# Four graph layers on one core: per-edge numbers summed with a stored 0/1 matrix in place of vector reductions and dots

## The chip, the core and the metric

The kernel runs on one core of a Trainium2 chip. The metric is the device time of one execution in microseconds (us), as the median of several runs; the profile is of one more execution. The engines are PE (matmul, with PEld for the weight loads), DVE (vector), ACT (scalar, activation functions), POOL (general purpose; it also issues the indirect DMAs) and SP (here it issues plain DMAs).

## What is computed

`x` has N = 2708 rows (nodes) of 512 features, `adj` is 2708 × 2708 with about five non-zero weights in a row (diagonal included). Four layers follow each other, each closed by a residual sum and a layernorm:

```python
# layer 0
x = layernorm(x + (x - (adj @ x) * (diag_1 + 1)) @ W + bias)
# layer 1: two gates, an attention over the edges
gate_a = sigmoid(concat([adj @ x, x]) @ Wa.T + ba)       # one number per row
gate_b = sigmoid(concat([adj @ x, x]) @ Wb.T + bb)
h = x @ W_sa
s = (h @ a_left)[:, None] + (h @ a_right)[None, :]       # one number per edge
e = where(adj != 0, exp(-leaky_relu(s, 0.01)), 0)
x_a = (e / (e.sum(1, keepdims=True) + 1e-5)) @ h
x_b = adj @ (x @ W_gcnb) + b_gcnb
x = layernorm(x + sigmoid(gate_a * x_a + gate_b * x_b))
# layer 2
head = (adj > 0) / max(norm of its row, 1e-12);  inc = adj + head
x = layernorm(x + (inc @ x) / inc.sum(1, keepdims=True))
# layer 3
A = adj + I;  d = A.sum(0) ** -0.5
x = layernorm(x + tanh((d[:, None] * A * d[None, :]) @ x @ W3.T + b3))
```

## The kernel before

The rows are worked on in 22 blocks of 128 (the last has 20); `xs` keeps all of x in SBUF, block by block. Everything takes place in `sparse_path` (a dense version runs only if the adjacency doesn't fit the sparse one). The edges of a block, up to 640, are put into five tiles of 128 edges. An edge has its value `ev`, its column `ej` (the row of x to fetch) and its row within the block `ec`; a sixth "tile" is the block's own rows, with the diagonal values.

`gather` (L606) fetches the 128 x-rows of each tile by one indirect DMA on POOL's queue: five a block in every layer, into a ring of eleven buffers. `one_hot` (L624) makes of a tile's edge numbers the matrix s[edge, row] = value where the row is the edge's, by one DVE instruction a tile, six a block. `aggregate` (L635) multiplies the six matrices with the gathered rows on PE (one 128x512 matmul each), and so sums the edges by row. `dot` (L640) is a DVE product with a row sum. `transposed` (L647, L649) is four PE transposes and an ACT copy, `project` (L654) four matmuls with a 512 × 512 weight, `layernorm` is L662 to L673, and `store` issues on SP, as the adjacency load (L701) does.

**Layer 0** also finds the edges. The loop at L903 to L915 works at three blocks at once: in pass `it` it loads adjacency block it+1 (double buffered, SP's queue), finds the non-zeros of block `it` (Max8 and FindIndex8, L766 and L767, with ACT's `minus` passes at L773, which test for negative values), moves the found numbers of block it−1 to edge tiles (`spread_rows`: matmuls `got` L829, ACT copies `rowsets` L839) and reads values and columns off them (`pick_edges`: `hit` L848, `prod` L852, `e` L859, far, num, `ej` L866, `row` L870), after which it issues the gathers, and projects block it−2: `l0a` (aggregate), `l0u` (L882, L883), transposes, `l0o` (POOL's `xb` L879 by the identity at L890, then `project`), layernorm, a dot with `wr` for the attention, and the store of x1 with that number behind it (`x1d`). After the loop come a test of the adjacency and the column degrees `deg` and `d_inv` (L942 to L966), which layer 3 needs.

**Layers 1 to 3** share the loop `layer` (L1078): gather block i+1, prepare its matrices, then compute block i and finish block i−1. In layer 1 `l1_prepare` (L984 to L1045) makes three dots of the block's rows, spreads the left attention number by a PE transpose (`sp`) and an ACT copy, picks it per edge with a 128x768 product and a row reduction (`tmp` L1001, L1010), adds the gathered right numbers, max, leaky ReLU, Exp, makes the second matrix `se`, and sums the columns of three such matrices (attention, value, count) by a `part` reduction over tiles (L1026, L1029, L1033) and three fp32 matmuls with ones (`sums` L1038). `l1_gates` (L1047) makes the two gates by dots on the aggregated rows; `l1_finish` projects (`l1o`, eight matmuls) and normalises.

Each engine runs its own list of instructions in order. The order in those lists is not the program text's: a scheduler arranges the instructions ahead of time by their dependencies, and a wait stands in front of an instruction wherever a buffer or an operand comes from another engine.

Of the kernel before, what the change touches and what calls it, by code (L numbers as in the profile page):

```python
# [480 lines left out]
def sparse_path(  # L481
# [11 lines left out]
    XW = D + 2  # L493
# [19 lines left out]
    x1d = dram.tile([N, XW], FP, name="x1d")  # L513
# [6 lines left out]
    n_xg = 11  # L520
    xg_buf = [const.tile([P, XW], FP, name=f"xg{k}") for k in range(n_xg)]
    for t in xg_buf:
        nc.gpsimd.memset(t, 0.0)
# [58 lines left out]
    ej = const.tile([P, NB, TILES], U32, name="ej")  # L582
    for i in range(NB):
        nc.gpsimd.tensor_copy(ec[:, i, n_tiles(i) : n_tiles(i) + 1], iota_p)
        nc.gpsimd.tensor_copy(ev[:, i, n_tiles(i) : n_tiles(i) + 1], dval[:, i : i + 1])

    junk = const.tile([P, D], FP, name="junk")
    wl_bc = const.tile([P, D], FP, name="wl_bc")
    wr_bc = const.tile([P, D], FP, name="wr_bc")
# [8 lines left out]
    n_gathers = [0]  # L598

    def gather(i, src, width):  # L600

        tiles = []
        for t in range(n_tiles(i)):
            g = xg_buf[n_gathers[0] % n_xg]
            n_gathers[0] += 1
            nc.gpsimd.indirect_dma_start(  # L606
                out=g[:, :width],
                out_offset=None,
                in_=src[:, :],
                in_offset=bass.IndirectOffsetOnAxis(ap=ej[:, i, t : t + 1], axis=0),  # L610
                bounds_check=N - 1,
                oob_is_err=False,
            )
            tiles.append(g)
        return tiles

    def one_hot(i, vals, tag, name, diag=None):

        r = rows(i)
        nt = n_tiles(i)  # L620
        s = spool.tile([P, TILES + 1, P], FP, tag=tag, name=name)
        for t in range(nt + 1):
            v = vals[:, t : t + 1] if diag is None or t < nt else diag
            nc.vector.tensor_scalar(  # L624
                s[:, t, :r], iota_c[:, :r], ec[:, i, t : t + 1], v, op0=ALU.is_equal, op1=ALU.mult
            )
        return s

    def aggregate(pool, i, s, tiles, tag, name):
        r = rows(i)  # L630
        nt = n_tiles(i)
        agg = pool.tile([P, D], FP, tag=tag, name=name)
        for t in range(nt + 1):
            rhs = tiles[t][:, :D] if t < nt else xs[:, i, :D]
            nc.tensor.matmul(agg[:r, :], lhsT=s[:, t, :r], rhs=rhs, start=(t == 0), stop=(t == nt))  # L635
        return agg
# [107 lines left out]

    found = c0.tile([P, NB, 3, SLOTS], FP, name="found")
    index = c0.tile([P, NB, SLOTS], U32, name="index")
    count = c0.tile([P, NB, SLOTS], FP, name="count")
# [3 lines left out]
    wlr = c0.tile([P, 2, DB], FP, name="wlr")  # L751
    for s, w_bc in enumerate((wl_bc, wr_bc)):
        ps = psa.tile([P, D], FP, tag="o", name=f"wlr_ps{s}")
        for f in range(DB):
            dot(wlr[:, s, f : f + 1], w_sa_sb[:, f, :], a_bc[:, s * D : (s + 1) * D], P)
            nc.tensor.transpose(
                ps[:, f * P : (f + 1) * P], wlr[:, s, f : f + 1].to_broadcast([P, P]), ident
            )
        nc.scalar.copy(w_bc, ps)

    def find(i, a, segs):
        for s in segs:
            lo, hi = SEGS[s]
            part = a[:, lo:hi, :].rearrange("p b i -> p (b i)")
            best = found[:, i, 1, 8 * s : 8 * s + 8]
# [3 lines left out]
    def find_first(i, a):  # L769
# [11 lines left out]
        find(i, a, range(0, 3))  # L781

    def find_rest(i, a):
        find(i, a, range(3, len(SEGS)))
        f = found[:, i]
# [3 lines left out]
            count[:, i, :], ones[:, :SLOTS], valid, 0.0, op0=ALU.mult, op1=ALU.add  # L789
# [10 lines left out]
        ps = psg.tile([P, 2], FP, tag="off", name=f"off_ps{i}")  # L800
        n = count[:, i, SLOTS - 1 : SLOTS]
        nc.tensor.matmul(ps[:, 0:1], lhsT=before, rhs=n, start=True, stop=True)
        nc.tensor.matmul(ps[:, 1:2], lhsT=before2, rhs=n, start=True, stop=True)
        off = w0p.tile([P, 2], FP, tag="off", name=f"off{i}")
        nc.scalar.copy(off, ps)
        return valid, off

    def spread_rows(i, prepared):

        valid, off = prepared  # L810
        nt = n_tiles(i)
        f = found[:, i]
# [5 lines left out]
            f[:, 0, :], count[:, i, :], off[:, 0:1], valid, op0=ALU.add, op1=ALU.mult  # L818
# [4 lines left out]
            count[:, i, SLOTS - 1 : SLOTS],  # L823
# [21 lines left out]
    def pick_edges(i, rowsets):  # L845
# [25 lines left out]
        nc.vector.tensor_copy(ec[:, i, :nt], row[:, :nt])  # L871
        nc.vector.tensor_copy(ev[:, i, :nt], e2[:, :nt, 0])
        tiles = gather(i, x, D)
        return one_hot(i, ev[:, i], "s", f"s0_{i}"), tiles
# [19 lines left out]
    def l0_norm(i, o):  # L894
        r = rows(i)
        layernorm(xs[:r, i, :D], o[:r, :], r, f"l0_{i}")
        dot(xs[:r, i, D : D + 1], xs[:r, i, :D], wr_bc[:r, :], r)
        store(x1d, i, xs[:r, i, :])
# [4 lines left out]
    for it in range(NB + 2):  # L903
# [3 lines left out]
        if it < NB:  # L907
            find_first(it, adj)
# [3 lines left out]
        if it < NB:  # L912
            prepared = find_rest(it, adj)
        if o is not None:
            l0_norm(it - 2, o)  # L915


    worst = small.tile([P, 4], FP, tag="worst", name="worst")
    nc.vector.memset(worst, 0.0)
    nc.vector.tensor_reduce(  # L920
        worst[:, 0:1],
        found[:, :, 1, :].rearrange("p i (s k) -> p i s k", k=8)[:, :, :, 7],
# [4 lines left out]
    tot = psg.tile([P, NB], FP, tag="off", name="tot")  # L927
    nc.tensor.matmul(tot, lhsT=ones, rhs=count[:, :, SLOTS - 1], start=True, stop=True)
    nc.vector.tensor_reduce(worst[:, 2:3], tot[:, :NF], AX.X, ALU.max)
    nc.vector.tensor_scalar(  # L930
        worst[:, 2:3], worst[:, 2:3], float(TILES * P), None, op0=ALU.is_gt
    )
    nc.vector.tensor_scalar(worst[:, 3:4], tot[:, NF : NF + 1], float(P), None, op0=ALU.is_gt)
# [3 lines left out]
    bad_ps = psg.tile([P, NB], FP, tag="off", name="bad_ps")  # L937
    nc.tensor.matmul(bad_ps[:, 0:1], lhsT=ones, rhs=bad[:, 1:2], start=True, stop=True)
    nc.vector.tensor_scalar(flag_i, bad_ps[0:1, 0:1], 0.0, None, op0=ALU.is_gt)


    deg = c0.tile([P, NB], FP, name="deg")  # L942
    block = c0.tile([P, NB, SLOTS], U32, name="block")
    nc.vector.tensor_scalar(block, index, 7, None, op0=ALU.logical_shift_right)
    part = c0.tile([P, NB, SLOTS], FP, name="deg_part")
    dsum = c0.tile([P, len(SEGS)], FP, name="dsum")
    for m in range(4):
        nc.vector.scalar_tensor_tensor(
            part, block, float(m), found[:, :, 1, :], op0=ALU.is_equal, op1=ALU.mult
        )  # L950
        nc.vector.tensor_reduce(
            dsum, part.rearrange("p i (s k) -> p s i k", k=8), AX.XY, ALU.add
        )
        for s, (lo, hi) in enumerate(SEGS):
            if lo + m < hi:
                nc.vector.tensor_copy(deg[:, lo + m : lo + m + 1], dsum[:, s : s + 1])
    nc.vector.scalar_tensor_tensor(deg, dval, 1.0, deg, op0=ALU.add, op1=ALU.add)

    zero = c0.tile([P, NB], FP, name="zero")
    nc.vector.tensor_scalar(zero, deg, 0.0, None, op0=ALU.is_equal)  # L960
    nc.vector.tensor_add(d_inv, deg, zero)
    nc.scalar.activation(d_inv, d_inv, AF.Sqrt)
    nc.vector.reciprocal(d_inv, d_inv)
    nc.vector.tensor_scalar(zero, zero, -1.0, 1.0, op0=ALU.mult, op1=ALU.add)
    nc.vector.tensor_mul(d_inv, d_inv, zero)
    nc.vector.scalar_tensor_tensor(dd3, dval, 1.0, d_inv, op0=ALU.add, op1=ALU.mult)  # L966
# [9 lines left out]
    wa2_bc = load_row(c1, wa, "wa2_bc", off=D)  # L976
    wb2_bc = load_row(c1, wb, "wb2_bc", off=D)
    ba_bc = load_row(c1, ba, "ba_bc", n=1)
    bb_bc = load_row(c1, bb, "bb_bc", n=1)
    wa1_bc = load_row(c1, wa, "wa1_bc")  # L980
    wb1_bc = load_row(c1, wb, "wb1_bc")
    bg_bc = load_row(c1, b_gc, "bg_bc")

    def l1_prepare(i, tiles):  # L984
        r = rows(i)
        nt = n_tiles(i)
        x1 = xs[:r, i, :D]
        loc = w1p.tile([P, 4], FP, tag="loc", name=f"loc{i}", bufs=3)
        dot(loc[:r, 0:1], x1, wl_bc[:r, :], r)
        dot(loc[:r, 1:2], x1, wa2_bc[:r, :], r)  # L990
        dot(loc[:r, 2:3], x1, wb2_bc[:r, :], r)
        sp = psm.tile([P, P], FP, tag="s", name=f"sp{i}")
        nc.tensor.transpose(
            sp[:, :r], loc[:r, 0:1].to_broadcast([r, P]), ident[:r, :r]
        )
        row = w1p.tile([P, P], FP, tag="row", name=f"row_sl{i}")
        nc.scalar.copy(row[:, :r], sp[:, :r])
        sv = one_hot(i, ev[:, i], "s", f"s1v{i}")
        m = nt + 1
        tmp = w1p.tile([P, TILES + 1, P], FP, tag="tmp", name=f"tmp{i}")  # L1000
        nc.vector.scalar_tensor_tensor(  # L1001
            tmp[:, :m, :r],
            sv[:, :m, :r],
            0.0,
            row[:, None, :r].to_broadcast([P, m, r]),
            op0=ALU.not_equal,
            op1=ALU.mult,
        )
        e = w1p.tile([P, 2, TILES + 1], FP, tag="e", name=f"e{i}")
        nc.vector.tensor_reduce(e[:, 0, :m], tmp[:, :m, :r], AX.X, ALU.add)  # L1010
        for t in range(nt):
            nc.vector.tensor_add(e[:, 0, t : t + 1], e[:, 0, t : t + 1], tiles[t][:, D : D + 1])
        nc.vector.tensor_add(e[:, 0, nt:m], e[:, 0, nt:m], xs[:, i, D : D + 1])
# [216 lines left out]
```

## Time and profile before

| | |
|---|---|
| median of 3 runs | 1303.86 us (1302.4 to 1307.16) |
| the profiled execution, its own time | 1311.38 us |
| its span in the trace | 1309.7 us |
| PE, DVE, ACT, POOL busy | 82%, 70%, 37%, 39% of the span |
| the chain that ended last | PE 49%, DVE 21%, DMA 20%, issue 6%, POOL 2%, ACT 2% |
| granted PE clock, mean | 0.931 |

The span runs from the first to the last instruction of the trace. Layer 0 takes it up to about 489 us, layer 1 to 925, layer 2 from 931 to 1090, layer 3 to the end. "Busy" is a share of the whole span; since the four layers have different limits, each has to be looked at by itself. A chain of waits is read from its end backwards: each piece is what the next one waited for.

### The profile page before, as it was taken

What the parts mean: (1) busy time and instruction counts of PE and PEld (TensorE: products, weight loads), DVE (VectorE), ACT (ScalarE), POOL (GpSimd) and SP (SyncE); (2) the same over time, 40 slices, a digit from 0 to 9 for tenths busy, and PEclk for the clock granted to TensorE, in tenths of its full rate; (3) what the DMA queues carried; (4) which work ended last, traced back from release to release, by engine and by line L of the source; (5) the groups of instructions that cost most, each with busy time, mean ns of one, the idle gap of its engine ahead of it and who ended that gap; (6) DMA issues with size and microseconds to landing.
All of it is one profiled execution on the core that took longest, in us unless ns stands there. A gap on an engine that the chain in (4) does not pass through costs nothing.

```text
span 1309.7 us, 11436 instructions
## 1 busy us (share of the span) xinstructions
PE 1080.0 (82%) x2868; PEld 490.4 (37%) x2868; DVE 912.5 (70%) x2710; ACT 487.7 (37%) x820; POOL 513.2 (39%) x566
## 2 busy tenths in 40 slices
PE   0377877777778758999999999999688886999996
PEld 0233333333333314444444444444223222444442
DVE  1877786777777987988888888874477772344443
ACT  0423323233232213545445445445212111565555
POOL 5333342333424325222222222210377775755540
PEclk9989988888787977999999999999799997999999
DMA  9544544535444224222212222210366664645530
GB/s 319 132 134 129 166 131 120 157 94 168 124 125 122 78 94 112 64 65 81 67 57 83 67 57 81 66 35 16 106 196 188 184 193 125 176 146 150 147 113 36
DMA packets 111155, 154.05 MB, mean 118 GB/s; under 512 B 17214, under 2 KB 74082, under 8 KB 111082
## 3 DMA queue, kind: packets, MB, share of 16 engines
q0 software_dynamic: 35952, 96.16, 25.7%
q1 hardware_dynamic: 72364, 51.55, 12.9%
q10 hardware_dynamic: 2766, 5.55, 1.3%
q8 instruction: 25, 0.41, 0.1%
q14 instruction: 48, 0.39, 0.1%
HBM read 152.96 MB, written 22.21 MB: 134 GB/s over the span
## 4 chain that ended last, share of the span: by engine, by line
PE 49%; DVE 21%; DMA 20%; issue 6%; POOL 2%; ACT 2%; POOLq 0%; ACTq 0%; SPq 0%
PE l3a L635 9%; PE l1o L654 8%; DMA xg<-in_x_dram,ej 7%; PE l1a L635 6%; DMA xg<-x2d,ej 6%; PE l3o L654 6%; PE l0a L635 6%; DMA adj<-in_adj_dram 5%; PE l1e L635 5%; DVE junk L640 3%; PE l2a L635 3%; DVE s1e L624 2%; DVE part L1026 2%; PE l0o L654 2%; DVE index L767 2%
## 5 line engine op out<-in xcount | busy, mean ns | idle before, releaser
L606 POOL DMA_INDIRECT xg<-x1d,ej x106 | 109.6, 1034 | 271.8 <-PE l1e L635 232.9
L635 PE MATMUL l0a<-xg,s 128*128 128x512 f32 x212 | 122.2, 687 | 38.2 <-DMA xg<-in_x_dram,ej 36.4
L606 POOL DMA_INDIRECT xg<-in_x_dram,ej x106 | 107.8, 1017 | 90.1 <-DVE row L870 52.8
L606 POOL DMA_INDIRECT xg<-x3d,ej x106 | 107.5, 1014 | 78.7 <-PE l3a L635 47.0
L635 PE MATMUL l2a<-xg,s2i 128*128 128x512 f32 x212 | 110.0, 637 | 29.3 <-DMA xg<-x2d,ej 28.8
L606 POOL DMA_INDIRECT xg<-x2d,ej x106 | 115.6, 1090 | 44.6 <-issue 16.8
L654 PE MATMUL l0o<-w_sb,uT_l 128*128 128x512 f32 (+1 forms) x176 | 116.0, 821 | 13.1 <-ACT uT_l L649 12.7
L635 PE MATMUL l3a<-xg,s 128*128 128x512 f32 x212 | 100.8, 608 | 10.6 <-DMA xg<-x3d,ej 10.6
L635 PE MATMUL l1a<-xg,s1v 128*128 128x512 f32 x212 | 97.8, 608 | 8.5 <-DMA xg<-x1d,ej 8.5
L766 DVE MAX8 found<-adj 128x8 f32<-128x512 f32 (+1 forms) x132 | 82.5, 637 | 31.6 <-DMA adj<-in_adj_dram 31.3
L635 PE MATMUL l1e<-xg,s1e 128*128 128x512 f32 x212 | 99.2, 598 | 0.0
L624 DVE TENSOR_SCALAR s<-iota_c,ec,ev 128x128 f32<-128x128 f32 x234 | 69.9, 364 | 34.9 <-PE l3a L635 34.9
L654 PE MATMUL l1o<-w_gc_sb,uT_l1a 128*128 128x512 f32 (+1 forms) x176 | 85.2, 612 | 0.0
L767 DVE FIND_INDEX8 index<-found,adj 128x8 uint32<-128x512 f32 (+1 forms) x132 | 84.0, 638 | 0.0
L654 PE MATMUL l3o<-w_sb,uT_l 128*128 128x512 f32 (+1 forms) x176 | 80.3, 600 | 0.3 <-ACT uT_l L649 0.3
L879 POOL TENSOR_TENSOR xb<-xs,b_bc 128x512 f32<-128x512 f32 (+1 forms) x22 | 29.8, 1355 | 127.1 <-PE l0o L890 127.1
L654 PE MATMUL l1o<-w_sa_sb,uT_l1e 128*128 128x512 f32 (+1 forms) x176 | 79.4, 593 | 0.0
L773 ACT ACTIVATE minus<-adj 128x1408 bf16<-128x1408 f32 x44 | 60.8, 1382 | 47.5 <-DMA adj<-in_adj_dram 46.6
L635 PEld LDWEIGHTS l2a<-xg,s2i 128*128 128x128 f32 x212 | 36.3, 195 | 94.7 <-DMA xg<-x2d,ej 65.7
L654 PEld LDWEIGHTS l0o<-w_sb,uT_l 128*128 128x128 f32 (+1 forms) x176 | 44.1, 263 | 72.2 <-issue 54.1
L635 PEld LDWEIGHTS l0a<-xg,s 128*128 128x128 f32 x212 | 38.2, 208 | 86.4 <-DMA xg<-in_x_dram,ej 62.4
L635 PEld LDWEIGHTS l1a<-xg,s1v 128*128 128x128 f32 x212 | 39.3, 194 | 56.8 <-issue 44.1
(213 smaller groups left out, 1923.4 us busy)
## 6 DMA issues: line engine op xcount, KB each, us to landing
adj<-in_adj_dram SPq DMA_DIRECT2D x21, 1344.0 KB
x1d<-xs SPq DMA_DIRECT2D x21, 257.0 KB
xs<-in_x_dram ACTq DMA_DIRECT2D x3, 1792.0 KB
x2d<-xs SPq DMA_DIRECT2D x21, 256.0 KB
x3d<-l2y SPq DMA_DIRECT2D x21, 256.0 KB
out_dram<-y SPq DMA_DIRECT2D x21, 256.0 KB
xg<-in_x_dram,ej POOLq DMA_INDIRECT x106, 5.4
xg<-x1d,ej POOLq DMA_INDIRECT x106, 3.4
```

The costliest lines, as they stand in the source:

```text
L606: nc.gpsimd.indirect_dma_start(out=g[:, :width], out_offset=None, in_=src[:, :], in_offset=bass.IndirectOffsetOnAxis(ap=ej[:, i, t : t + 1 ...
L624: nc.vector.tensor_scalar(s[:, t, :r], iota_c[:, :r], ec[:, i, t : t + 1], v, op0=ALU.is_equal, op1=ALU.mult)
L635: nc.tensor.matmul(agg[:r, :], lhsT=s[:, t, :r], rhs=rhs, start=(t == 0), stop=(t == nt))
L640: nc.vector.scalar_tensor_tensor(junk[:r, :], a, 1.0, b, op0=ALU.mult, op1=ALU.mult, accum_out=acc)
L654: nc.tensor.matmul(o[:r, :], lhsT=uT[:, f, :r], rhs=w[:, f, :], start=start and f == 0, stop=stop and f == DB - 1,)
L766: nc.vector.max(out=best, in_=part)
L767: nc.vector.max_index(index[:, i, 8 * s : 8 * s + 8], best, part)
L773: nc.scalar.activation(minus, a[:, k * half : (k + 1) * half, :], AF.Relu, scale=-1.0, accum_out=neg[:, i, k : k + 1],)
L879: nc.gpsimd.tensor_tensor(xb[:r, :], xs[:r, i, :D], b0_bc[:r, :], ALU.add)
L1026: nc.vector.tensor_reduce(part[:, 0, :r], se[:, :m, :r].rearrange("p t i -> p i t"), AX.X, ALU.add)
```

## The change

1. **A stored 0/1 matrix.** In layer 0 each block's `pick[edge, row]` (bf16, 1 where the edge belongs to the row) is made once, by one DVE is_equal over 128x640, and kept for all layers. `weighted` takes the place of `one_hot`: one DVE product of `pick` with the five columns of edge values (128x640), and one ACT copy of the identity scaled by the diagonal values.
2. **Numbers per row.** After layer 0's layernorm the block is transposed and multiplied with a 512 × 6 weight: right attention number, the two gates' numbers for the aggregated side, left attention number, the two gates' numbers for the own side (`l0_columns`). `x1d` carries the first three behind the row, `sld` is a second store with the left number alone. The dot with `wr` goes.
3. **Layer 1 per edge.** Five more indirect DMAs a block fetch the left number of each edge's row (4 bytes each) by the index `er`. The attention, the value, the count and the value times each gate number are five numbers per edge; they are split into three bf16 parts and summed by row with five matmuls of `pick` (128x15). The gates, row sums and counts come out of that, before the block is aggregated.
4. The gather buffers are two of five tiles each in place of a ring of eleven; `deg` and `d_inv` are worked out at the start of layer 1; the copy of the found values goes to ACT; the total that the adjacency test needs comes from the offsets rather than from a matmul; some tags move to other pools.

```diff
-    xg_buf = [const.tile([P, XW], FP, name=f"xg{k}") for k in range(n_xg)]
+    xg_buf = [const.tile([P, TILES, XG], FP, name=f"xg{k}") for k in range(2)]
+    sl_buf = [const.tile([P, TILES], FP, name=f"sl{k}") for k in range(2)]
...
+    pick = const.tile([P, NB, TILES, P], BF, name="pick")
...
     def gather(i, src, width):
+        g = xg_buf[i % 2]
         for t in range(n_tiles(i)):
+            gather_rows(g[:, t, :width], src, ej[:, i, t : t + 1])
+        return g
...
-    def one_hot(i, vals, tag, name, diag=None):
...
-        for t in range(nt + 1):
...
-            nc.vector.tensor_scalar(
-                s[:, t, :r], iota_c[:, :r], ec[:, i, t : t + 1], v, op0=ALU.is_equal, op1=ALU.mult
-            )
+    def weighted(i, vals, pool, name, diag=None):
...
+        nc.vector.tensor_tensor(
+            s[:, :nt, :r],
+            pick[:, i, :nt, :r],
+            vals[:, :nt, None].to_broadcast([P, nt, r]),
+            ALU.mult,
+        )
+        nc.scalar.activation(
+            s[:, nt, :r],
+            ident[:, :r],
+            AF.Copy,
+            scale=vals[:, nt : nt + 1] if diag is None else diag,
+        )
...
+        nc.vector.tensor_scalar(er[:, i, :nt], row[:, :nt], float(i * P), None, op0=ALU.add)
...
         tiles = gather(i, x, D)
-        return one_hot(i, ev[:, i], "s", f"s0_{i}"), tiles
+        nc.vector.tensor_tensor(
+            pick[:, i, :nt, :],
+            iota_c[:, None, :].to_broadcast([P, nt, P]),
+            ec[:, i, :nt, None].to_broadcast([P, nt, P]),
+            ALU.is_equal,
+        )
+        return weighted(i, ev[:, i], spool, f"s0_{i}"), tiles
...
-        dot(xs[:r, i, D : D + 1], xs[:r, i, :D], wr_bc[:r, :], r)
-        store(x1d, i, xs[:r, i, :])
+    def l0_columns(i):
+        r = rows(i)
+        xT = transposed(psg, xs[:, i, :D], r, f"x1_{i}")
+        cols = psg.tile([P, 6], FP, tag="off", name=f"cols{i}")
+        for f in range(DB):
+            nc.tensor.matmul(
+                cols[:r, :], lhsT=xT[:, f, :r], rhs=w6[:, f, :], start=f == 0, stop=f == DB - 1
+            )
+        nc.scalar.copy(xs[:r, i, D:], cols[:r, :])
+        store(x1d, i, xs[:r, i, :XG])
+        store(sld, i, xs[:r, i, XG : XG + 1])
...
     def l1_prepare(i, tiles):
...
+        l1_gather(i)
+        q = w1p.tile([P, 3, TILES + 1], FP, tag="q", name=f"q{i}")
+        nc.vector.tensor_copy(
+            q[:, :, :nt], tiles[:, :nt, D:XG].rearrange("p t k -> p k t")
+        )
...
+        nc.vector.tensor_add(att[:, :nt], q[:, 0, :nt], sl_buf[i % 2][:, :nt])
...
+        nc.scalar.activation(att, att, AF.Exp, scale=-1.0)
...
+        nc.vector.tensor_copy(e3[:, 0, :, :nt], e[:, :, :nt])
+        nc.vector.tensor_sub(rest[:, :, :nt], e[:, :, :nt], e3[:, 0, :, :nt])
+        nc.vector.tensor_copy(e3[:, 1, :, :nt], rest[:, :, :nt])
+        nc.vector.tensor_sub(e3[:, 2, :, :nt], rest[:, :, :nt], e3[:, 1, :, :nt])
+        ps = psm.tile([P, 15], FP, tag="s", name=f"sums{i}")
         for t in range(nt):
+            nc.tensor.matmul(
+                ps[:r, :],
+                lhsT=pick[:, i, t, :r],
+                rhs=e3[:, :, :, t].rearrange("p c k -> p (c k)"),
+                start=t == 0,
+                stop=t == nt - 1,
+            )
...
+        sv = weighted(i, ev[:, i], spool, f"s1v{i}")
+        se = weighted(i, e[:, 2], w1p, f"s1e{i}")
+        return sv, se, g
```

In the lists that the scheduler makes of the changed kernel, DVE has hit, prod, e, far and num of block k+1 ahead of l0u of block k (before, prod and e stood behind or between l0u's two instructions); PE has the transposes of x1 (`tr_x`) and the `cols` matmuls of block k−1 among the six aggregation matmuls of l0a(k); in layer 1 PE has sums(k+1) between the first and second tile of l1e(k), ahead of l1o(k−1).

## The prediction

> **What bounds the kernel now.** I read the page's chain first, then windows inside each layer, then the chain of waits in layer 0 and PE's timeline in layer 1. Windows of layers 0, 1, 2, 3 (after the times: busy us and instructions of each engine, granted clock, DMA share, GB/s):
>
> ```profile
> core 0: us, PE busy (x) PEld busy (x) DVE busy (x) ACT busy (x) POOL busy (x), PEclk, DMA share, GB/s
> 300.00:340.00 40.00, 30.97 (x80) 14.53 (x80) 30.55 (x95) 12.06 (x22) 14.61 (x14) 0.83 0.45 133
> 560.00:720.00 160.00, 155.96 (x453) 74.17 (x451) 135.68 (x386) 74.29 (x132) 42.12 (x42) 1.00 0.24 70
> 930.00:1090.00 160.00, 127.74 (x272) 46.65 (x272) 110.65 (x301) 28.72 (x62) 116.17 (x107) 0.95 0.61 175
> 1110.00:1280.00 170.00, 169.99 (x449) 77.30 (x448) 72.22 (x218) 98.64 (x128) 95.10 (x94) 1.00 0.50 144
> ```
>
> No engine fills layer 0; PE fills layers 1 and 3. In layer 2 five gathers a block, 1.09 us each plus .30 between, make the 6.95 us of a block on POOL. The chain in layer 0 shows a ring (start, us, what):
>
> ```profile
> 315.80 6.54 DMA xg<-in_x_dram,ej
> 322.34 0.04 issue
> 322.38 2.05 PE l0a L635 x4
> 324.43 1.23 PE got L829 x10
> 325.66 1.73 PE l0a L635 x4
> 327.39 0.02 issue
> 327.41 0.69 DVE l0u L882
> 328.10 0.56 DVE prod L852
> 328.67 1.67 DVE l0u L883
> 330.34 0.56 DVE e L859
> ...
> 332.70 0.07 DVE ej L866
> 332.77 0.08 DVE row L870
> ```
>
> Landed gather, l0a, l0u, prod, e, ej, then POOL issues the next block's gather: prod and e of block k+1 stand behind l0u of block k, which waits for l0a(k). So gather k+1 never starts before l0a(k) has ended. The adjacency loads are 20.58 us apart over twelve blocks.
>
> Layer 1, PE's timeline:
>
> ```profile
> 758.70 0.83 PE L1038 MATMUL sums<-ones,part 128*128 128x1 f32 x6 [0.78 <-DVE part L1026]
> 759.39 1.11 PE L654 MATMUL l1o<-w_gc_sb,uT_l1a 128*128 128x512 f32 x2
> 760.33 3.60 PE L654 MATMUL l1o<-w_sa_sb,uT_l1e 128*128 128x512 f32 x8
> ```
>
> Its blocks are 19.53 us apart; PE's only real stop is the sums' wait for the part reduces on DVE.
>
> **Layer 0: the order.** In after's order on DVE, hit, prod, e, far and num of block k+1 come before l0u(k); ej comes with it. From the end of l0a(k), ej is .69 + .15 away (before: 332.77 − 327.39 = 5.4). Its gather then takes, from 332.77 to the landing, about 1.5 on POOL and 6.5 of DMA: 9 us after l0a(k). That is no longer last. Last is now PE's other path: l0u .69 + .7 to 1.67, transposes .6, uT copy .6 to .7, l0o 5.2 at this clock (l3o, the same four steps at clock 1.00, takes 3.43 a block: 4.1 at .83; the identity's step adds 1.0), got 1.23: 9.0 to 10.1 us, take 9.5. If the clock rose to 1.00 it would be .9 less. Then l0a itself: 6 × .87 to .95 = 5.4.
>
> **Layer 0: what is added.** PE's order puts the new x1 transposes (.5, as for the other four) and the cols matmuls (about .4) into l0a: tr_x after tile 1, cols after tile 2. tr_x waits for the layernorm of block k−1: st .70, mv .18, three small steps of .15 to .30, the ACT pass .6, 2.3 us after l0o, while got and two l0a tiles hide 3.1. cols wait for an ACT copy of .7, one l0a tile hides .9. If ACT is late (it also has minus, rowsets and the diagonal copy in its queue) each stop costs up to 1 us. Period: 9.5 + 5.4 + .9 + 1.4 for such stops = 17.2. Bounds: 15.5 with no stops; 20, if both stops come each time and DVE is late too.
>
> DVE's own sum: six one_hot steps go (net .255 each start to start, 1.51), the wr dot goes (.68), two 128x640 tensor_tensors come. The trace has 128x512 at .69 and 128x768 at .946, so 640 is about .82, net .73 to .75; with er (.15) that is −.6 of 15.5 busy (30.55 over 1.95 blocks): 14.9, under 17.2. A price against it: L883, with two SBUF inputs, takes 1.67 in this window and .69 (L882, one input from PSUM) just before it, when POOL runs xb. pick and the weights are such instructions too. The Trainium skill (SBUF — State Buffer, Who interferes with whom) says that a DVE instruction with two SBUF inputs contends with a GpSimd instruction that reads SBUF, by an exclusive lock. By that rule one of them could lose up to another 1.0 a block, an estimate that would make the period 18.2 and 12 us of the gain vanish; I take the trace's sum, since xb runs once a block and L883 already pays for it.
>
> Gain: twelve blocks × (20.58 − 17.2) = 41, three early ones (18.6 apart) × 1.4 = 4; the last five, already 13.6 apart, nothing. −45; bounds −8 (period 20) to −70 (15.5).
>
> **Between the layers.** deg and d_inv, 4 × 1.240 + 4 × 1.238 + block .69 + copies, some 12 us of DVE, move from layer 0's tail behind the first gathers of layer 1, where DVE waits for landings (489.3 to 493.1) and then for PE. Added at the tail: transposes, copy, cols, copy, about 2, and the sld store beside x1d's. If deg ends after the first attention chain is due, it costs up to 8. I take −3, bounds −8 to +6. At the start, w6's four strided loads go out on ACT's queue ahead of minus: 0 to +4, I take 0, since minus first waits for adjacency anyway (46.6 of ACT's idle).
>
> **Layer 1.** Gone from DVE: five dots (.61 to .68), three part reduces (1.46), three tmp passes (.96, .95, .55), twelve one_hots; added: two weights of .82 and some 22 small ones of .07 to .2. DVE's 16.6 a block falls to about 7 (16.6 − 3.4 − 4.4 − 2.5 − 3.1 + 1.6 + 2.2). PE loses sp and the sums' six fp32 passes (.66), gains five narrow bf16 matmuls (.3 to .6). PE's own work: l1a and l1e 5.15 each, l1o 6.87, transposes .86, sums .4: 18.4.
>
> But a ring appears. There are two gather buffers of five tiles (ten tiles, before eleven), and sums(k+2) stand in PE's order before l1o(k). Tile 1 of gather k+2 waits for l1e(k) tile 1, which comes just after l1o(k−1). From the end of l1o(k−1): tile 1 .86; three more gathers to the last, 3 × 1.31 = 3.93; landing 3.4; then on DVE q, add, max, leaky, mult, the three-way split, with both weights of .82 in between, and Exp on ACT (about .4): 2.2 + 1.6 + .4 = 4.2; sums .4; l1o(k) 6.87. Sum 19.7. Against 19.53: 21 × .2 = +4. Bounds: landing 2.2 and no weight in the way gives the PE floor 18.4, −24; landing 4.8 and Exp's table load (1.283 in the trace) on the path gives 22.4, +60. I take +4.
>
> The five 4-byte gathers of sl: POOL gets 10 × 1.31 = 13.1 of 19.7. They wait for add(k), then queue ahead of gather k+1's tiles, whose PE wait ends later still: 2.3 us of slack, so nothing; without that slack they delay tile 1.
>
> **Layers 2 and 3.** The weights replace six one_hots by one .82 on DVE and a .264 diagonal copy on ACT. POOL sets layer 2 and PE layer 3 (169.99 of 170); the cover is 49 us of idle DVE in 160 and 98 in 170. If it were gone, 44 × .2 = 9. Zero. The copy of value on ACT, offs for tot and the tags that move to other pools cost small instructions of .15 in the tail at most: zero.
>
> **Sum.** −45 − 3 + 4 = −44. The profiled execution took 1311.38 (span 1309.7), .6% over the median 1303.86; −44 on the first is 1267, on the median 1260. I give 1260.
>
> **Rivals.**
> A. Layer 0's ring closes elsewhere: tr_x, cols, or an adjacency load issued late because SP stands behind x1d and sld stores keep the period at 20 or more. For it: PE's work a block, 15.9 by the window, leaves little at clock .83. Against: adjacency has .45 of the DMA engines and room. Then −8 − 3 + 4: 1297, about no change.
> B. Slower: the layer 1 ring, one mechanism. sums(k+2) ahead of l1o(k) make PE wait for every late landing. Layer 0's gathers land in 5.4, the first in 6.5, where other transfers run. At 5.4 to 6.5 with Exp's load on the path the period is 23 to 24.1: +73 to +96 less 48, 1329 to 1352. It decides from a period of 21.8 on (48 / 21 above 19.53), and is slower by .5% from 22.1; B holds all above that, from 1311. For it: PE has no other work queued behind sums. Against: landings of 3.4 at DMA share .24.
> C. Both good: 16.4 in layer 0 and the PE floor in layer 1: −55 − 3 − 24, 1222.
> D. The freed DVE time was all cover, no ring opens: 1304. Against it: PE idles 9 of 40 us in layer 0's window, behind a ring whose DVE links move.
>
> **How the numbers follow.** The forecast (1240 to 1285) .52; A .14, half within .5%; B .19; C .12; D .03. About .5%, 6.5 us, is what a measurement of this kernel can tell from no change. Faster .52 + .12 + .07 = .71, same .07 + .03 = .10, slower .19. The range goes from C, 1222, into the lower part of B, 1318: .06 of C and .13 of B stay outside.
>
> **What would show it.** Right: adjacency issues 16 to 18.5 apart, the ring's ej within 1 us of l0a's end, l1o 19 to 20.5 apart with PE waiting before sums. Wrong: adjacency still 20 apart; PE idle over 2 us a block before sums; POOL over .8 busy in layer 1; or DVE idle and PE waiting for cols.

## The result, and the profile after

The changed kernel takes 1354.74 us (1346.33 to 1368.52), the kernel before 1305.51 in the same comparison: a ratio of 1.034, interval 1.024 to 1.044. It is slower by 3.4%, where 1260 and 3.4% faster was forecast. The ratio compares fast runs alone and leaves out the slow one of 1368.52. The profiled execution took 1346.33 us, with a span of 1344.5 against 1309.7.

The first reading is where the 34.8 us of span went. First and last starts of the named matmuls in the two traces give the stages:

| us | before | after | difference |
|---|---|---|---|
| start to last l0o | 478.2 | 503.3 | +25.1 |
| last l0o to first l1a | 14.9 | 13.7 | −1.2 |
| first l1a to first l1o | 25.9 | 40.6 | +14.7 |
| first to last l1o | 400.6 | 398.7 | −1.9 |
| last l1o to the end | 390.1 | 388.2 | −1.9 |

So layers 2 and 3 and the steady part of layer 1 are as forecast, within 6 us; layer 0, which was to give 45, lost 25, and the start of layer 1 lost 15. The windows that answer to those of before, same stretches (layer 2's runs later now, so its third window holds the last blocks of layer 1 too, and the fourth the change from layer 2 to 3):

```profile
300.00:340.00 40.00, 30.78 (x100) 16.14 (x101) 27.66 (x83) 15.14 (x34) 14.40 (x15) 0.90 0.63 141
560.00:720.00 160.00, 153.15 (x434) 69.86 (x434) 54.00 (x239) 74.45 (x132) 88.40 (x87) 0.99 0.24 67
930.00:1090.00 160.00, 132.63 (x299) 46.90 (x298) 87.01 (x168) 44.47 (x91) 95.50 (x89) 0.96 0.52 150
1110.00:1280.00 170.00, 157.60 (x404) 70.58 (x403) 55.94 (x126) 88.72 (x127) 99.94 (x99) 0.96 0.52 150
```

Layer 1's line shows what was meant: DVE falls from 135.68 to 54.00 us. Layer 0's line has the surprise in its last two columns. The DMA engines were busy .45 of the time at 133 GB/s; now they are busy .63 at 141. More time, hardly more bytes. The waits of PE in layer 0 say who suffers (what waited for what: us in total, times, longest). Before:

```profile
PE l0a L635 <- DMA xg<-in_x_dram,ej: 36.4, 28, 3.3
PE tr_l L647 <- DVE l0u L883: 30.4, 15, 2.7
```

After:

```profile
PE l0a L647 <- DMA xg<-in_x_dram,ej: 77.8, 19, 9.7
PE l0o L666 <- ACT uT_l L661: 14.5, 13, 2.9
PE tr_x L659 <- ACT xs L685: 13.9, 8, 5.1
PE tr_l L659 <- DVE l0u L907: 7.9, 11, 1.9
```

The wait that the change was to open, PE behind DVE's l0u, did go, from 30.4 to 7.9. In its place PE waits for gathers, up to 9.7 us at a time. And the gathers are not issued late; they land late. In the DMA view of one stretch in the middle of layer 0, 230 to 345 us (queue, packets, MB, share of 16 engines; q0 carries the gathers, q1 adjacency and stores), before has

```profile
q1 hardware_dynamic: 17268, 9.90, 29.6%
q0 software_dynamic: 2400, 6.45, 18.7%
```

and after

```profile
q0 software_dynamic: 2400, 6.48, 42.2%
q1 hardware_dynamic: 17240, 9.45, 30.9%
```

The same 2400 packets with the same bytes hold the engines 2.26 times as long. Counted in the trace's packet records, 422 packets took over 1.5 us each in the whole of after (the longest 8.6), 2 in before; 345 of them are on the gathers' queue (8 of these of a weight load behind the last gathers) and 76 are adjacency rows, all by the end of layer 0. In layer 1, which reads with ten small and large gathers a block, there are none. The one new thing that is on the DMA engines in layer 0 alone is the second store of each block: `sld`, 128 numbers of 4 bytes, one beside the other in memory. The packet records point at it too: all 421 long packets of the two queues start within 9.8 us after the first packet of a block's `sld` store (half of them within 4.2), and blocks are some 20 us apart.

### The profile page after: what moved, and what is told of

It is laid out like the page before. It is cut to its first block, busy times and chain, and to the rows that moved or that the text cites. A ratio compares the mean times of both kernels' runs of the same rounds, so it can differ in the third digit from the quotient of the medians.

```text
span 1344.5 us, 11455 instructions
## 1 busy us (share of the span) xinstructions
PE 1077.4 (80%) x3074; PEld 496.0 (37%) x3074; DVE 660.4 (49%) x2008; ACT 529.2 (39%) x953; POOL 618.5 (46%) x661
## 3 DMA queue, kind: packets, MB, share of 16 engines
q1 hardware_dynamic: 75418, 51.57, 14.3%
## 4 chain that ended last, share of the span: by engine, by line
PE 26%; DMA 16%; issue 15%; POOL 10%; DVE 5%; ACT 2%; POOLq 0%; DVEq 0%; ACTq 0%; SPq 0%
PE l3a L647 8%; DMA xg<-x2d,ej 7%; PE l3o L666 6%; DMA xg<-x1d,ej 5%; POOL xg L606 5%; POOL sl L606 5%; PE l1o L666 3%; PE l0a L647 2%; DMA xg<-in_x_dram,ej 2%; PE l2a L647 2%; PE l0o L666 2%; PE l1e L647 1%; PE l1a L647 1%; PE tr_l L659 1%; DMA xg<-x3d,ej 1%
## 5 line engine op out<-in xcount | busy, mean ns | idle before, releaser
L647 PE MATMUL l0a<-xg,s 128*128 128x512 f32 x212 | 127.3, 722 | 84.0 <-DMA xg<-in_x_dram,ej 77.8
L606 POOL DMA_INDIRECT xg<-in_x_dram,ej x106 | 115.2, 1087 | 151.9 <-DVE row L887 59.6
L606 POOL DMA_INDIRECT sl<-sld,er x106 | 109.9, 1037 | 80.5 <-DVE e L1012 53.3
L647 PE MATMUL l3a<-xg,s 128*128 128x512 f32 x212 | 100.7, 606 | 11.2 <-DMA xg<-x3d,ej 11.2
L666 PE MATMUL l0o<-w_sb,uT_l 128*128 128x512 f32 (+1 forms) x176 | 89.0, 653 | 14.9 <-ACT uT_l L661 14.5
L647 PEld LDWEIGHTS l0a<-xg,s 128*128 128x128 f32 x212 | 41.4, 222 | 121.5 <-DMA xg<-in_x_dram,ej 48.9
L1070 DVE SCALAR_TENSOR_TENSOR l1v<-bg_bc,g,l1o 128x512 f32<-128x512 f32 (+1 forms) x22 | 16.4, 747 | 104.6 <-PE l1o L666 104.6
L647 PEld LDWEIGHTS l1a<-xg,s1v 128*128 128x128 f32 x212 | 40.2, 192 | 62.9 <-issue 47.5
L647 PEld LDWEIGHTS l3a<-xg,s 128*128 128x128 f32 x212 | 38.9, 193 | 55.3 <-issue 46.5
```

The source lines that it names most:

```text
L606: nc.gpsimd.indirect_dma_start(out=dst, out_offset=None, in_=src[:, :], in_offset=bass.IndirectOffsetOnAxis(ap=index, axis=0), bounds_chec ...
L666: nc.tensor.matmul(o[:r, :], lhsT=uT[:, f, :r], rhs=w[:, f, :], start=start and f == 0, stop=stop and f == DB - 1,)
L1070: nc.vector.scalar_tensor_tensor(v[:r, :], bg_bc[:r, :], g[:r, 1:2], o[:r, :], op0=ALU.mult, op1=ALU.add)
```

## The experiments

Theory S is that these four-byte stores hold up the packets of other transfers. Q is that SP's order does it: in seven blocks of after the second part of an adjacency load stands behind x1d's and sld's stores, which wait for cols. P is that the x1 transposes and cols inside l0a, with ACT's fuller queue, are the price. All times are medians, all ratios are to the kernel before on the same chip; where that took 1320.62 rather than 1304 to 1307, only the ratio is told.

**1. One store of sld after layer 0.**

```diff
-        store(sld, i, xs[:r, i, XG : XG + 1])
...
+        nc.sync.dma_start(
+            out=sld[: NF * P, :].rearrange("(b p) o -> p (b o)", p=P), in_=xs[:, :NF, XG]
+        )
+        nc.sync.dma_start(out=sld[NF * P :, :], in_=xs[:TAIL, NF, XG : XG + 1])
```

> The changed kernel, but the left numbers are stored to sld by one DMA after layer 0's loop instead of 128 four-byte rows beside every block's x1d store. Theory S (the four-byte stores hold up other packets in the DMA engines): in the changed kernel's trace 422 packets of gathers and adjacency loads take over 1.5 us (2 in the kernel before), all in layer 0; here they are gone, a layer 0 gather lands in 6 us or less instead of 9.2 in the median, layer 0 gets 25 to 60 us shorter, the time falls to 1290 to 1325. Rival Q (SP's order: the second part of an adjacency load stands behind an x1d store that waits for cols): nothing of that is changed, so gathers may land earlier but the adjacency period stays at 20 us, the time within 10 us of 1350. Rival P (PE's and ACT's order, x1 transposes and cols inside l0a): same, within 10 us of 1350.

1283.44, ratio 0.982 (0.976 to 0.988): a loss of 3.4% became a gain, a little larger than S gave. Long packets fell from 422 to 23, and 22 of these are of a weight load, from 439 to 446 us, 6 to 13 us behind the last packet of the one late store (433.0); the last l0o starts at 434.7 rather than 503.3. SP's order is as it was (a store between the two parts of an adjacency load), and so is PE's. Q and P, which both expected 1350, fall.

**2. The kernel before, with such a store and nothing else.**

```diff
         store(x1d, i, xs[:r, i, :])
+        store(sld, i, xs[:r, i, D : D + 1])
```

> The kernel before with one thing added: each block of layer 0 also stores one number of each row (4 bytes times 128) to a tensor that nobody reads. Theory S: packets over 1.5 us go from 2 to some hundreds, layer 0's gathers land in 8 to 10 us instead of 5.4, and since the gather is on layer 0's ring before the change, each of 22 blocks gets 2 to 4 us longer: 1350 to 1390. Rivals Q and P: 22 more stores of .4 us on SP, which has room: 1304 to 1310, landings as before.

1332.04, ratio 1.019 (1.015 to 1.023). The store alone slows the old kernel. The size is less than expected: 96 long packets, and the last l0o is 19.3 us later, .9 us a block rather than 2 to 4. The gather's line in layer 0 shows why the median misleads:

```profile
DMA to landing us min/median/max: 2.2/6.0/12.4
```

Before, the same line of the same stretch (60 to 490 us) has

```profile
DMA to landing us min/median/max: 2.4/5.4/6.9
```

and after

```profile
DMA to landing us min/median/max: 2.7/9.4/15.0
```

The 90 long packets of the two queues here start within 8.5 us after a store of sld. In the old kernel few gathers are caught; in the changed one the median lands later than the latest of before. Why (in before the stores keep one distance from the gathers, in after they drift) is argued, not shown.

**3. The left number inside x1d's rows, no sld at all.**

```diff
+    XR = XG + 1
+    x1d = dram.tile([N, XR], FP, name="x1d")
...
-        store(x1d, i, xs[:r, i, :XG])
-        store(sld, i, xs[:r, i, XG : XG + 1])
+        store(x1d, i, xs[:r, i, :XR])
...
-            gather_rows(sl[:, t : t + 1], sld, er[:, i, t : t + 1])
+            gather_rows(sl[:, t : t + 1], x1d[:, :].rearrange("n (c o) -> (n c) o", o=1),
+                er[:, i, t : t + 1], N * XR - 1)
```

> The changed kernel without the tensor sld: the left number is the 516th number of a row of x1d, and the five small gathers of layer 1 fetch 4 bytes out of x1d by a flat index. No four-byte store at all. Theory S: as e1_sld_once, 1290 to 1325, and equal to it within 8 us. Should the rows' odd length of 2060 bytes be what slows the packets (2064 here), only this one gets faster and e1_sld_once does not. Rivals Q and P: within 10 us of 1350.

1270.11, ratio 0.971 (0.967 to 0.975), no long packet, landings 2.2/3.8/7.0. It is better than S expected, and better than one late store by 13 us, where at most 8 were expected. Most of that is the store of 2708 four-byte rows between the layers: last l0o to first l1a takes 20.1 us there and 11.2 here. The odd length of the rows plays no part, as e1, with 2060 bytes, gained too.

**4. Stores on ACT's queue.**

```diff
-    def store(dst, i, src):
+    def store(dst, i, src, eng=None):
...
-        nc.sync.dma_start(out=dst[i * P : i * P + r, :], in_=src)
+        (eng or nc.sync).dma_start(out=dst[i * P : i * P + r, :], in_=src)
...
-        store(x1d, i, xs[:r, i, :XG])
-        store(sld, i, xs[:r, i, XG : XG + 1])
+        store(x1d, i, xs[:r, i, :XG], nc.scalar)
+        store(sld, i, xs[:r, i, XG : XG + 1], nc.scalar)
```

> The changed kernel with x1d's and sld's stores issued by ACT right after the copy that makes their last numbers, so that SP holds adjacency loads alone and none of them stands behind a store. Rival Q: the adjacency period falls from 20.2 to 17 or 18, the time falls by 20 to 45 us, to 1305 to 1330. Theory S: the four-byte stores are still there beside the gathers, packets over 1.5 us stay in the hundreds, the time stays within 12 us of 1350. Rival P: no change either.

1342.64, ratio 1.031 (1.025 to 1.037), 345 long packets. SP now holds adjacency loads alone, and nothing is won. Q is out a second time.

**5 and 6. Small, or side by side?** Two layouts of sld: four bytes at a distance of 64, and 64 bytes side by side. The small gathers' index is changed to fit.

```diff
+    SW = 16
-    sld = dram.tile([N, 1], FP, name="sld")
+    sld = dram.tile([N, SW], FP, name="sld")
...
-        store(sld, i, xs[:r, i, XG : XG + 1])
+        store(sld[:, 0:1], i, xs[:r, i, XG : XG + 1])      # e5_pitch64
+        store(sld, i, xs[:r, i, XW - 16 : XW])             # e6_rows64
```

> The changed kernel with sld laid out as 16 numbers a row and only the first of them stored: the four-byte stores stay, but lie 64 bytes apart rather than side by side (sld is filled with zeros once at the start). Theory S1 (the stores are slow because they are small): packets over 1.5 us stay in the hundreds, gathers of layer 0 land in 8 to 10 us, 1335 to 1360. Theory S2 (they are slow because neighbours write into the same short stretch of memory from different DMA engines): the long packets go, 1265 to 1290.

> The changed kernel with sld's store widened to the last 16 numbers of a row, 64 bytes side by side in memory; the left number is one of them. As many rows and DMAs as in the changed kernel, sixteen times the bytes. S1: how small is too small is open; if 64 bytes are enough, 1265 to 1290 and no long packets, otherwise 1335 to 1360. S2: each row has a stretch of its own, so 1265 to 1290. With e5_pitch64: both fast means S2, only this one fast means S1, both slow means S1 with a larger bound.

Ratios 0.983 (0.977 to 0.990) and 0.980 (0.974 to 0.987), one long packet of 1.6 us in each. Both are fast, so of the two it is S2: the size of a store is not what hurts. e5 sends, beside one fill at the start, exactly the 2708 four-byte packets of the changed kernel, to other addresses. The gathers' queue in the stretch of 230 to 345 us now has

```profile
q0 software_dynamic: 2912, 7.83, 24.6%
```

which is more packets than in the changed kernel in little over half the engines' time. That the neighbours must come from different DMA engines, as S2 has it, no run separates.

**7 and 8. The same on the kernel before,** the store of experiment 2 at 64 and at 32 bytes' distance:

```diff
-    sld = dram.tile([N, 1], FP, name="sld")
+    sld = dram.tile([N, 16], FP, name="sld")      # e13; [N, 8] in e14
...
-        store(sld, i, xs[:r, i, D : D + 1])
+        store(sld[:, 0:1], i, xs[:r, i, D : D + 1])
```

> The kernel before with the four-byte store of e2_before_sld, but 64 bytes from row to row. As many packets of as many bytes as there, to other addresses. S2 (neighbouring numbers are what holds the DMA engines up): no long packets, 1.00 of the kernel before within .007, where e2_before_sld was 1.019. If it stays at 1.015 or more, the added stores themselves or their place in SP's queue cost the time.

> As e13_before_sld_pitch with 32 bytes from row to row rather than 64. If the numbers hold the DMA engines up whenever two rows share 64 bytes, long packets are back, fewer than with 4 bytes' distance since two rows meet rather than sixteen: 1.003 to 1.019 of the kernel before. If what is shared is 32 bytes or less, no long packets and 1.00 within .007.

1.000 (0.997 to 1.003) and 1.002 (0.999 to 1.006), with 2 and 1 long packets. Twenty-two more stores cost nothing that can be measured; twenty-two that write neighbouring numbers cost 1.9%. At 32 bytes the neighbours don't meet either. Whether 8 or 16 bytes are enough, and whether it is the neighbours or the unbroken run of 512 bytes that four-byte rows make up, wasn't tried.

**9. The start of layer 1, without the small gathers.** e3 still takes 40.2 us from the first l1a to the first l1o. Theory R: the small gathers in POOL's queue. Rival T: deg on DVE.

```diff
-        store(sld, i, xs[:r, i, XG : XG + 1])
...
+        nc.tensor.transpose(
+            sp[:, :r], xs[:r, i, XG : XG + 1].to_broadcast([r, P]), ident[:r, :r]
+        )
...
+        nc.scalar.copy(left[:, :r], sp[:, :r])
...
+        nc.vector.tensor_tensor(
+            tmp[:, :nt, :r],
+            pick[:, i, :nt, :r],
+            left[:, None, :r].to_broadcast([P, nt, r]),
+            ALU.mult,
+        )
...
+        nc.vector.tensor_reduce(sl[:, :nt], tmp[:, :nt, :r], AX.X, ALU.add)
...
-        l1_gather(i)
+        sl = l1_left(i)
```

> No sld and no small gathers: layer 1 picks each edge's left number on DVE, as pick times the block's left numbers spread over a row (a PE transpose and an ACT copy), and a row reduction over 128x640; neither waits for a gather. Theory R (the late start of layer 1, 40 us from the first l1a to the first l1o where the kernel before took 26, is the five small gathers of 1.31 us that stand in POOL's queue among the large ones): against e3_sl_in_x1d, 1270, the start gets 8 to 14 us shorter, l1o stays 19 to 19.5 apart because the ring over the two gather buffers stays: 1254 to 1264. Rival T (the start is late because deg and d_inv, 12 us of DVE, stand there): the start stays at 38 to 42 us, 1266 to 1276.

> e10_left_on_dve once more beside e12_left_deg_late, since that chip ran every kernel some 1.2% slower: a ratio to the kernel before of 0.955 to 0.968.

Ratios 0.956 (0.949 to 0.962) and, run again, 0.955 (0.952 to 0.958): 1248.70 against 1306.86, the best of the study. The start takes 32.9 us, 7.3 less than e3's (8 to 14 were expected) and 7.0 more than before's: about half of the loss is R's. First to last l1o takes 391.4 us in the second run, 6.3 less than in e3; whether the small gathers had cost that in the steady part is open, since the next run, without them too, takes 397.9. POOL's timeline of the changed kernel shows the queue that is gone here: the second block's gather starts only behind the five small ones (start, us, engine, line).

```profile
519.45 1.01 POOL L606 DMA_INDIRECT xg<-x1d,ej  x1 [0.30 <-issue]
520.76 1.00 POOL L606 DMA_INDIRECT sl<-sld,er  x1 [0.30 <-issue]
...
526.51 1.00 POOL L606 DMA_INDIRECT sl<-sld,er  x1 [0.30 <-issue]
527.82 1.01 POOL L606 DMA_INDIRECT xg<-x1d,ej  x1 [0.30 <-issue]
```

**10. deg behind layer 1.** The twelve us of deg and d_inv are moved, unchanged, behind the call of layer 1.

> As e10_left_on_dve, with deg and d_inv written behind layer 1 in the program, so that they fill gaps of DVE instead of standing ahead of the first attention chain. e10_left_on_dve took 33 us from the first l1a to the first l1o, the kernel before 26, e3_sl_in_x1d 40. If deg makes what is left of the late start (rival T in part), it falls to 26 to 29 and the time is 4 to 7 us under e10_again; if the start hangs on POOL's gathers of 1.31 us alone, nothing changes within 2 us.

The start takes 29.0 us instead of 33.0 (e10_again): PE's wait there for s1e, a matrix that DVE makes, falls from 9.4 us to 1.6. So T holds for 4 of the 7 us that the start was still late. But the time is the same, where 4 to 7 us less were expected: 0.957 (0.954 to 0.960) beside 0.955 (0.952 to 0.958). In the two profiled executions layer 0 ends 5.9 us earlier here, and first to last l1o takes 6.5 us longer; why the gain at the start doesn't reach the end is open. So are the last 3 us of the late start. One candidate, argued from DVE's timeline in e10 only: a copy of block 1's gathered numbers stands ahead of block 0's chain there and waits 3.6 us for its gather.

**11. A third gather buffer.**

```diff
-    xg_buf = [const.tile([P, TILES, XG], FP, name=f"xg{k}") for k in range(2)]
+    xg_buf = [const.tile([P, TILES, XG], FP, name=f"xg{k}") for k in range(3)]
...
-        g = xg_buf[i % 2]
+        g = xg_buf[i % 3]
...
-            junk[:r, :], a, 1.0, b, op0=ALU.mult, op1=ALU.mult, accum_out=acc
+            xg_buf[0][:r, 0, :D], a, 1.0, b, op0=ALU.mult, op1=ALU.mult, accum_out=acc
```

The last two lines spare the buffer `junk`: the eight dots that make the 512 × 6 weight write what nobody reads into a gather buffer.

> As e10_left_on_dve with three gather buffers of five tiles rather than two. The prediction's ring in layer 1 (tile 1 of gather k+2 waits for l1e(k), sums(k+2) stand before l1o(k)) is open: gather k+2 waits for l1e(k-1). If that ring sets layer 1's period, l1o come 18.3 to 18.6 apart rather than 19.3, 15 to 20 us less than e10_left_on_dve: 1235 to 1248. If PE's order or the clock sets it, within 5 us of e10_left_on_dve.

Ratio 0.967 (0.960 to 0.975), beside e10's 0.956 (0.949 to 0.962) on the same chip: neither of the two times expected, but slower. The ring of two buffers is not what paces layer 1 to a worthwhile degree: first to last l1o takes 387.4 rather than 390.3 us. Layer 0 ends 9.5 us earlier, the start of layer 1 takes 4.0 us longer, and layers 2 and 3 take 12.2 us longer (last l1o to the end 415.6 against 403.4, at clock .96 against .98 from 1060 to 1225 us). Why is open, and not all of that need be the third buffer's: e10's own kernel took 388.8 in that stretch on another chip (e10_again).

## Why the prediction was wrong

**Layer 0: the order came as described, and its sum was near, in part by luck.** e3 has the change with sld gone and everything else kept. There layer 0 ends 47.6 us earlier than in before; 45 was forecast. The step "the ring's ej no longer waits" is borne out: in e3's DVE timeline from 268 to 345 us, ej of block k+1 starts between 2.6 us before and .6 us after l0u(k), where in before's chain it starts 5.3 us after it (332.70 against 327.41). The waits say the same. e3's PE waits in layer 0 are

```profile
PE l0a L647 <- DMA xg<-in_x_dram,ej: 17.6, 7, 9.7
PE tr_x L659 <- ACT xs L685: 12.6, 8, 2.8
PE l0a L647 <- DVE index L781: 10.9, 3, 4.3
PE l0o L666 <- ACT uT_l L661: 10.2, 13, 1.9
PE tr_l L659 <- DVE l0u L909: 8.9, 13, 1.9
```

36.4 on gathers became 17.6, 30.4 on l0u 8.9, and the two stops that were priced, tr_x and cols, come to 12.6 and 1.1. New, and in no term of the sum, are the 10.9 us that end with DVE's search for non-zeros (`index`). The cols matmuls themselves take .87 a block in e3's chain, where .4 was put.

The period of 17.2 did not come as a steady one. Adjacency loads are 16.7 us apart in e3 (89.47 to 356.28 over 16 blocks), but 18.2 in the first eight blocks and 15.1 in the last eight. By the first l0o matmul with the weight in each block, e3 gains nothing on before up to the eighth block (208.1 against 209.0 us) and then takes 16.2 us a block against 20.5. So the early blocks gave nothing, where 4 us were forecast, and the last five gave 9, where nothing was. The sum was made at clock .83; e3's clock is .87 from 89 to 235 us and .97 from 235 to 356. That doesn't explain the two stages: e10_again has them too (19.3, then 16.2 us a block) at .92 in both stretches. What holds the first blocks is open. In the second stretch of e3 DVE is busy 112.48 of 121 us, so its own sum, put at 14.9 a block and off the path, is as near to the limit as PE's path.

**The step that failed** is one clause in "Between the layers": "and the sld store beside x1d's", priced at nothing, and rival A, where sld appears as something that SP stands behind. It got no number of its own: by its issue (.42 us on SP) and its bytes (512 a block) it looks like nothing. Its price lay in what it does to others: e3 against the changed kernel is a ratio of 0.971 against 1.034, some 80 us for a transfer of .5 KB a block. No row of the trace of before could have given that number; the sound thing would have been to bound it, since before had no store of rows under 2 KB on these queues, and to let a rival carry it. Rival A's sign did come, adjacency loads 20.2 us apart in after (89.84 to 412.40 over 16 blocks), but not by its cause: with the stores off SP's queue (e4) nothing was won.

**A rule that points near it.** The prediction did not use it. The Trainium skill (DMA: Bandwidth & Descriptors, Specifications) gives 512 bytes as the least transfer for full rate, with read-modify-write below. That speaks against four-byte stores, but not as it came out: 4 bytes at 32 and at 64 bytes' distance and rows of 64 bytes, all below it, cost nothing measurable here. The measurement puts the trouble in neighbouring addresses.

**DVE's price for two SBUF inputs: right in kind, and nearly gone.** L883 took 1.478 us in the median in before; the same instruction takes .684 after, where xb seldom runs beside it. In layer 0 of after one pick of 22 took over 1 us (1.473; the median is .817) and three of the weights (up to 2.179; .819), where 13 of L883's 22 did in before. The sum by the trace's rows held. The twelve us that could have come of the Trainium skill's rule (SBUF — State Buffer, Who interferes with whom) didn't show. The rule agrees with these rows, but only few of the new instructions meet xb.

**Layer 1: the number was near where it was steady, but not by the ring, and the start was missed.** First to last l1o took 397.7 us in e3, 2.9 less than before, for a forecast of +4: 18.9 us a block, where the ring over the gather buffers gave 19.7. PE's idle before sums, 14.0 us in 17 blocks, is there as described. But e11, which opens the ring, took only 2.9 us off e10's 390.3, and PE is busy 315.99 us of 330 in e3 (520 to 850 us): PE's own work sets the pace, and the ring's sum came near it by its sizes. The term that was missed is the start: 14.3 us more from the first l1a to the first l1o. The working priced the small gathers by their slack in the steady state ("2.3 us of slack, so nothing") and did not ask for the first blocks, where nothing hides POOL's 5 × 1.31 us a block; that is 7.3 of the 14.3 (e10, net of the work on DVE that takes their place). Another 4 are deg's (e12), which "it costs up to 8" had named and left out of the sum, and 3 are open. "−3" for the change of layers was right as far as the first l1a: 3.7 less in e3.

**Sum.** e3 has −47.6 − 3.7 + 14.3 − 2.9 − 1.1 = −41.0 us of span against a forecast of −44. The total fits the change without its four-byte stores, with the errors above partly cancelling: layer 0 gave 2.6 more than forecast and layer 1, its start included, 7.4 less. The chances did not fit: .71 for faster rested on traffic being priced by its own duration.

## What to carry to other kernels

In this kernel a new transfer had to be priced by what shares its engines, not by its bytes: when packets of unchanged number and size hold the DMA engines longer, something else on them is at fault, and the shares of the queues in one stretch show it in two lines. A single number a row is better carried as one more column of a wide row that is stored anyway, or put at a distance from its neighbours. And a queue that has slack in the steady state has none in the first blocks of a stage; a ramp needs a sum of its own.

## What the runs showed of the hardware

- A DMA of 128 rows of 4 bytes to neighbouring addresses holds up packets of other transfers for up to 8.6 us (422 packets over 1.5 us, 1.38 ms of packet time in all, in layer 0 of the changed kernel), though the four-byte packets of that queue are recorded with 9 ns in the median and 20 at most. The hold-up outlasts the store's own packets: long packets start up to 9.8 us after its first one. With 32 or 64 bytes from row to row, or with rows of 64 bytes, at most two packets in a whole run were over 1.5 us.
- An indirect DMA costs POOL the same 1.00 us in the median and .30 between, whether it fetches 128 rows of 4 bytes or of 2060.
- Taking the DVE load of layer 1 from 135.68 to 54.00 us of 160 moved its time by half a per cent (first to last l1o 400.6 to 398.7 us): PE was busy 153 to 156 us of the same window before and after.
